# Scores in float32r from high parts and rests, with the maxima subtracted by a product with ones, in an attention block between two feed-forward layers

## The chip, the cores and the metric

The kernel runs on one core of a Trainium2 chip, as one program. The metric is the device time of one execution in microseconds. The core has five engines that run beside each other, each through its own instructions in order: TensorE (PE, matrix products, with weight loads PEld), VectorE (DVE), ScalarE (ACT), GpSimd (POOL) and SyncE (SP), which here only issues DMA transfers. They wait for each other, and where need be for themselves, through counting semaphores. Products go to PSUM; everything else lies in SBUF, 128 partitions wide.

Times on the page and below are those of one profiled execution; the medians are over several runs without a profiler.

## What is computed

The input x is 16 batches of 256 tokens of 256 features, in float32. A feed-forward layer with ternary weights, an attention layer with 16 heads of 16 dimensions and rotary positions, and the feed-forward layer again are added to it:

```python
q = (x @ Wq.T).reshape(B, S, N_HEADS, HEAD_DIM).transpose(0, 2, 1, 3)
...
q = _apply_rope(q)
k = _apply_rope(k)
scores = jnp.einsum('bhqd,bhkd->bhqk', q, k) / np.sqrt(HEAD_DIM).astype(np.float32)
scores = jnp.where(causal, scores, -jnp.inf)
attn = jax.nn.softmax(scores, axis=-1)
out = jnp.einsum('bhqk,bhkd->bhqd', attn, v)
...
x = x + 0.5 * _L0_ffn_ref(_layernorm(x, axis=-1), ...)
x = x + _L0_attn_ref(_layernorm(x, axis=-1), L0_attn_Wq, L0_attn_Wk, L0_attn_Wv, L0_attn_Wo)
x = x + 0.5 * _L0_ffn_ref(_layernorm(x, axis=-1), ...)
```

The weights of q and k are drawn with a large factor, so scores are large, and the softmax needs its maxima subtracted and its scores nearly at float32's precision.

## The kernel before, in words

**Stages.** x stays in SBUF throughout (`xs`). `ffn(0, ...)` runs the first layer in 66 steps of four tiles of tokens. Then the attention runs batch by batch, and `ffn(2, ...)` is the second layer. The feed-forward products already use float32r: an operand is split into a high part that float32r holds exactly and a rest, and each is multiplied in turn (`turn_in`, `up`, `down`).

**Order.** The order of all work is written out by hand: `InOrder` (L188) keeps each engine's instructions in the order of the program, so nearly all of the profile's lines read L196. A batch of attention is eight calls of `slot(b, p)`, p from 0 to 7 (L687), one for each pair of heads. In each slot several batches are in work: `scores(bw, p, bm, p ^ 1)` computes the weights' scores of batch b - 1 (`w`) and, for the maxima, those of batch b (`m`). Batch b + 1 is being projected and rotated (`project_qk`, `rotate`, on POOL), older ones are multiplied with the values (`attend`), divided and projected out. Batch 0's slots lie among the last steps of the first feed-forward layer; a last loop (L815) computes w alone for batch 15, while the second layer begins.

**Scores.** Each score is computed twice. `m` has queries on PSUM's partitions; on it, VectorE's reduction (L592) finds each query's maximum over the allowed keys, with the sign turned, into one column of `maxes`, and drops the masked scores themselves into a scratch tile `masked` of the pool `proj`, which has two buffers of it. A reduction is two instructions: the operation and a read of the accumulator. `w` has keys on the partitions; it becomes exp(scores) after VectorE has added a causal mask (L608) and ScalarE has taken the exponential (L611). m takes one PSUM bank for each of a slot's two heads, from a pool of two; w takes two banks of a pool of two times two.

**Layout of q and k.** The head's 16 dimensions stand in a group of 32 rows, so that a product uses a quarter of TensorE's rows, and four heads' products may stand beside each other. `spread` (L504) copies a rotated q or k into its 32 rows through ScalarE with a column of zeros and ones as scale: heads of even and odd groups use the lower and the upper 16 rows. One of the unused rows carries the maxima: k has ones there (`one`), and q the negated maximum, put there by two transfers after `turn_max` (L528) has turned `maxes` with TensorE and copied it to `mT`. So the product of 32 rows is score minus maximum at once. These are float32 products, which TensorE takes in several passes; the trace shows two instructions for each.

**Queues.** SP issues, for each batch, two transfers for each of two halves that swap neighbouring rows for the rotation (`pair` from `raw`, L493) and two for each half's maxima (L537). POOL multiplies by cosine and sine, adds (L496 to L502), prepares the next batch's normalized x (`ready_x`, in p = 7) and multiplies by the reciprocal sums (`divide`, in p = 1 and p = 5), whose result `o` VectorE transposes a slot later (`turn_out`).

Of the kernel before, what the change touches and what calls it, by code (L numbers as in the profile page):

```python
# [23 lines left out]
S = 256  # L24
# [6 lines left out]
def kernel(  # L31
# [38 lines left out]
    w2q = const.tile([P, NFC, D], FR, name="w2q")  # L70


    wqk = const.tile([P, KC, 2, 2, 4, 2, HD], FP, name="wqk")
# [28 lines left out]
    for k in range(KC):  # L102
        rows = slice(k * P, (k + 1) * P)
        nc.sync.dma_start(out=wv[:, k, :], in_=wqkvT[rows, 2 * D :])
        for at in range(0, 2 * D, 4 * HD):
            n, j, e = at // D, at // P % 2, at // (4 * HD) % 2
            nc.sync.dma_start(
                out=wqk[:, k, n, j, :, e, :],
                in_=wqkvT[rows, at : at + 4 * HD].rearrange("p (r d) -> p r d", d=HD),
            )  # L110
    for at in range(0, P, HD):
        r, n = at // 32, at // HD % 2
# [7 lines left out]

    ident = const.tile([P, P], FP, name="ident")
    make_identity(nc, ident)

    averaging = const.tile([P, P], FP, name="averaging")
    nc.gpsimd.memset(averaging, 1.0 / (D * FF))
# [51 lines left out]

    maxes = [state.tile([P, 2, 2, P], FP, name=f"maxes_{i}") for i in range(2)]  # L180
    for v in maxes:
        nc.gpsimd.memset(v, 0.0)


    mv = [state.tile([P, NTILE, 2], FP, name=f"mv_{i}") for i in range(3)]
# [85 lines left out]
    cosT = const.tile([P, S], FP, name="cosT")  # L271
    sinT = const.tile([P, S], FP, name="sinT")

    own = [const.tile([P, 1], FP, name=f"own_{e}") for e in range(2)]
    one = [const.tile([P, 1], FP, name=f"one_{e}") for e in range(2)]

    def make_tables():
        tp = ps_mm.tile([P, 2, S], FP, name="mm")
        for n, table in enumerate((cos_sb, sin_sb)):
            wide = small.tile([P, 2, P // HD, HD], FP, name="wide", bufs=2)  # L280
            gpsimd.tensor_copy(wide, table.unsqueeze(2).to_broadcast([P, 2, P // HD, HD]))
            for c in range(2):
                tensor.transpose(
                    tp[:, n, c * P : (c + 1) * P],
                    wide[:, c, :, :].rearrange("p h d -> p (h d)"),
                    ident,
                )
        scalar.copy(cosT, tp[:, 0, :])
        scalar.copy(sinT, tp[:, 1, :])
        columns = ident.rearrange("p (r e d) -> p r e d", e=2, d=HD)  # L290
        for e in range(2):
            vector.tensor_reduce(own[e], columns[:, :, e, :], AX.XY, ALU.add)
            vector.tensor_reduce(one[e], columns[:, :, 1 - e, 0:1], AX.XY, ALU.add)

# [150 lines left out]
        later.extend(todo)  # L445


    xn_a, xnT, qT, kT, o, oT, y_a = {}, {}, {}, {}, {}, {}, {}
    pT, sums = {}, {}


# [2 lines left out]
        for k in (0, 4 * S)  # L454
    )
    qk = [flat2[:, at : at + 2 * S].rearrange("p (n s) -> p n s", n=2) for at in (0, 2 * S)]

    def ready_x(b, engine=gpsimd):
        xn_a[b] = pp.tile([P, 2, D], FP, name="xn_a", bufs=1)
# [16 lines left out]
    def project_qk(b, j, first=0, end=4):  # L476

        if first == 0:
            begun[b, j] = ps_mm.tile([P, 2, S], FP, name="mm")
        to = begun[b, j]  # L480
        for n, k in [(n, k) for n in range(2) for k in range(KC)][first:end]:
            tensor.matmul(
                to[:, n, :],
                wqk[:, k, n, j].rearrange("p r e d -> p (r e d)"),
                xnT[b][:, k, :],
                start=(k == 0),
                stop=(k == KC - 1),
            )
# [12 lines left out]
        if 2 in parts:  # L501
            gpsimd.tensor_add(qk[j], qk[j], pair[j])  # L502

    def spread(b, j, e):  # L504


        if (j, e) == (0, 0):
            qT[b] = hp.tile([P, 4, S], FP, name="qT", bufs=3)
            kT[b] = hp.tile([P, 4, S], FP, name="kT", bufs=3)
        g = 2 * j + e  # L510
        scalar.activation(qT[b][:, g, :], qk[j][:, 0, :], AF.Identity, scale=own[e])
        scalar.activation(
            kT[b][:, g, :], qk[j][:, 1, :], AF.Identity, bias=one[e], scale=own[e]
        )

    def project_v(b, c):
        v = ps_mm.tile([P, D], FP, name="mm")
# [7 lines left out]
            )  # L525
        scalar.copy(vals[b % 2][:, c, :, 0:HD], v.rearrange("p (h d) -> p h d", d=HD))

    def turn_max(b, j):  # L528

        tp = ps_mm.tile([P, S], FP, name="mm")  # L530
        for c in range(2):
            tensor.transpose(tp[:, c * P : (c + 1) * P], maxes[b % 2][:, c, j, :], ident)
        mT = hp.tile([P, S], FP, name="mT")
        scalar.copy(mT, tp)
        for e in range(2):
            rows = slice(HD * (1 - e), P, 32)
            sync.dma_start(out=qT[b][rows, 2 * j + e, :], in_=mT[rows, :])  # L537

    def scores(bw, pw, bm, pm):

# [12 lines left out]
        if masked:  # L553
            for j in range(2):
# [5 lines left out]
                    stop=False,  # L560
                    skip_group_check=True,
                )
        for c in range(2):
            for j in range(2):
                if w is not None:
                    h = 2 * pw + j
                    rows, g = slice(32 * (h % 4), 32 * (h % 4) + 32), h // 4
                    tensor.matmul(
                        w[:, j, c * S : S + c * P],
                        kT[bw][rows, g, c * P : (c + 1) * P],  # L570
                        qT[bw][rows, g, c * P : S],
                        start=(c == 0 and not masked),
                        stop=(c == 1),
                        skip_group_check=masked,
                    )
                if m is not None:
                    h = 2 * pm + j
                    rows, g = slice(32 * (h % 4), 32 * (h % 4) + 32), h // 4
                    tensor.matmul(
                        m[j][:, c * P : c * P + (c + 1) * P],  # L580
                        qT[bm][rows, g, c * P : (c + 1) * P],
                        kT[bm][rows, g, 0 : (c + 1) * P],
                        start=(c == 0),
                        stop=(c == 1),
                    )
        if m is not None:
            for j in range(2):
                h = 2 * pm + j
                at = 32 * (h % 4) + HD * (1 - h // 4 % 2)
                for c in range(2):  # L590
                    cols = (c + 1) * P
                    vector.tensor_tensor_reduce(  # L592
                        out=pp.tile([P, S], FP, name="masked")[:, 0:cols],
                        in0=m[j][:, c * P : c * P + cols],
                        in1=mask_q[:, S - cols : S],
                        scale=-1.0,
                        scalar=-MASKED,
                        op0=ALU.add,
                        op1=ALU.min,
                        accum_out=maxes[bm % 2][:, c, h // 8, at : at + 1],  # L600
                    )

        def weigh():
# [11 lines left out]
    def attend(b, half):  # L615

        av = ps_mm.tile([P, 2, S], FP, name="mm")
        for n in range(2):
            g = 2 * half + n
            for c in range(2):  # L620
                for r in range(4):
                    tensor.matmul(
                        av[32 * r : 32 * r + 32, n, c * P : S],
                        vals[b % 2][:, c, 4 * g + r, :],
                        pT[b, 2 * g + r // 2][:, r % 2, c * S : S + c * P],
                        start=(c == 0),
                        stop=(c == 1),
                    )
        sums[b, half] = av
# [57 lines left out]
    def slot(b, p, more=lambda: None):  # L687
# [25 lines left out]
            rotate(up, p // 2 - 1, *((1, 2) if p % 2 else (0,)))  # L713
        if p == 4 and past is not None:
            attend(past, 0)
        if p == 6 and b + 2 < NB:
            turn_x(b + 2)
        if p == 7:
            if last is not None and b < NB - 1:
                project_out(last, range(1, 2))  # L720
            if b + 2 < NB:
                project_qk(b + 2, 0, 0, 1)
            if b + 3 < NB:
                ready_x(b + 3)
            if up is not None:
                spread(up, 0, 0)
        more()
        weigh()
        for n, half, at in ((last, 1, p), (past, 0, p - 4)):
# [24 lines left out]
        50: lambda: (rotate(0, 1, 0), spread(0, 0, 0)),  # L754
        52: lambda: (rotate(0, 1, 1), spread(0, 0, 1)),
        55: lambda: rotate(0, 1, 2),
        56: lambda: ready_x(2, vector),
    }
    HEAD = 59
# [28 lines left out]
    for p in range(8):  # L788
# [11 lines left out]


    ahead = {
        0: lambda: project_out(NB - 3),
        1: lambda: turn_max(z, 1),
    }
    behind = {
# [77 lines left out]
```

## Time and profile before

| | us |
|---|---|
| median of 3 runs | 599.89 |
| lowest and highest | 598.81, 600.18 |
| the profiled execution | 599.31 |
| its span on the page | 597.5 |
| first feed-forward layer alone | from the start to about 140 |
| reductions of the maxima, batch 0 | 141.4 to 163.9 |
| reductions of the maxima, batches 1 to 15 | 164.6 to 447.7 |
| second feed-forward layer | from about 448 on |

The core's TensorE clock is granted in full throughout (the row PEclk is 9 in all slices, the windows say 1.00).

The costliest groups of the parts that the change touches, each as count, total us and mean ns of one (the page's part 5, with different shapes kept apart):

| engine and operation | count | us | mean ns |
|---|---|---|---|
| DVE reduction, masked from m, 128x256 | 240 | 100.7 | 420 |
| DVE reduction, masked from m, 128x128 | 240 | 68.0 | 283 |
| DVE read of the accumulator into maxes | 512 | 42.4 | 83 |
| PE matmul w from qT, kT, 32 rows, 256 columns | 512 | 91.9 | 426 |
| PE matmul w from qT, kT, 32 rows, 128 columns | 512 | 51.2 | 270 |
| PE matmul m from kT, qT, 256 columns | 480 | 75.5 | 377 |
| PE matmul m from kT, qT, 128 columns | 480 | 62.9 | 321 |
| ACT activation, kT | 64 | 37.9 | 593 |
| ACT activation, qT | 64 | 32.3 | 504 |
| POOL multiplication by cosT, 128x512 | 32 | 41.3 | 1289 |

How to read it: a matmul's time is from its start to a modelled end, and those that follow start long before; for what a block of matmuls takes, look from its first start to the start of what comes next. On VectorE too an operation may start before the one ahead has written its last element. "Idle before" in a group is the time in which its engine had nothing, and the name behind the arrow is what ended it.

### The profile page before, as it was taken

Reading aid. Unit: us, or ns where it says so; the run is one execution under the profiler, and the core shown is the slowest. Engines: PE = TensorE matmul, PEld = TensorE weight load, DVE = VectorE, ACT = ScalarE, POOL = GpSimd, SP = SyncE. Lnnn points to the kernel's source line nnn. Section 1 sums busy time; section 2 is a strip of 40 time slices with the busy share of each in tenths; the row PEclk is TensorE's granted clock in tenths of the full one; section 3 lists DMA queues with packets and bytes.
Section 4 is the critical chain, followed back from the end, with each engine's and each line's share of the span. In section 5 each row is a group of like instructions: output and inputs, shape, how many; then the busy total and the mean of one; then the engine's idle time right before and its main releaser. Section 6 shows DMA issues by size and latency. Waiting matters only on the chain.

```text
span 597.5 us, 14414 instructions
## 1 busy us (share of the span) xinstructions
PE 580.0 (97%) x5398; PEld 467.2 (78%) x5398; DVE 473.5 (79%) x1690; ACT 391.1 (65%) x668; POOL 324.8 (54%) x301
## 2 busy tenths in 40 slices
PE   4999999999999999999999999999999999999996
PEld 3798989887777777777777777777767788888886
DVE  6877888677688999899899999999986466666743
ACT  4576666675476666766667676676765666666664
POOL 4645665693555576555855668464821454455452
PEclk9999999999999999999999999999999999999999
DMA  8810000000010011100110001100000011111101
GB/s 282 196 27 2 1 1 1 36 1 19 19 39 20 20 38 37 37 23 20 38 38 28 31 19 38 38 20 28 31 4 2 2 36 36 36 36 36 35 30 41
DMA packets 25588, 21.26 MB, mean 36 GB/s; under 512 B 11056, under 2 KB 21168, under 8 KB 25520
## 3 DMA queue, kind: packets, MB, share of 16 engines
q1 hardware_dynamic: 24960, 19.44, 10.3%
q8 instruction: 42, 0.69, 0.5%
q10 hardware_dynamic: 560, 0.92, 0.4%
q14 instruction: 26, 0.21, 0.1%
HBM read 7.51 MB, written 4.19 MB: 20 GB/s over the span
## 4 chain that ended last, share of the span: by engine, by line
PE 88%; DVE 5%; ACT 3%; issue 1%; DMA 1%; POOL 1%; DVEq 0%; SPq 0%; POOLq 0%; ACTq 0%
PE mm L196 35%; PE w L196 31%; PE m L196 23%; DMA w<-in_w1T_dram 1%; DVE xn L196 1%; ACT h_high L196 1%; DVE masked L196 1%; ACT h_whole L196 1%; DVE w2q L196 1%; DVE h_rest L196 1%; DVE w L196 1%; DVE st L196 0%; POOL h_rest L196 0%; DVE x L196 0%; ACT pT L196 0%
## 5 line engine op out<-in xcount | busy, mean ns | idle before, releaser
L196 DVE CUSTOM_DVE_ANT_0 masked<-m,mask_q 128x128 f32<-128x128 f32 x480 | 142.1, 351 | 20.6 <-PE m L196 19.7
L196 PE MATMUL m<-xnT,w1q 128*128 128x512 f32 x504 | 143.3, 405 | 0.9 <-ACT xnT L196 0.7
L196 ACT ACTIVATE pT<-w 128x768 f32<-128x768 f32 x128 | 104.1, 814 | 56.3 <-DVE w L196 55.9
L196 ACT ACTIVATE h_high<-m,b_sb 128x512 fp32r<-128x512 f32 x126 | 86.7, 688 | 79.4 <-PE m L196 79.3
L196 DVE TENSOR_TENSOR h_rest<-h_whole,h_high 128x512 fp32r<-128x512 f32 x83 | 74.7, 900 | 60.3 <-ACT h_whole L196 59.9
L196 PE MATMUL w<-w2q,h_high 128*128 128x256 f32 x480 | 120.7, 285 | 0.3 <-DVE w2q L196 0.3
L196 PE MATMUL w<-qT,kT 32*128 32x256 f32 (+1 forms) x1024 | 120.5, 348 | 0.0
L196 PE MATMUL w<-w2q,h_rest 128*128 128x256 f32 x480 | 118.0, 279 | 0.8 <-POOL h_rest L196 0.7
L196 PEld LDWEIGHTS w<-qT,kT 32*128 32x128 f32 x1024 | 90.3, 184 | 33.6 <-issue 22.8
L196 PE MATMUL m<-kT,qT 32*128 32x128 f32 x960 | 115.0, 349 | 0.3 <-ACT kT L196 0.3
L196 POOL TENSOR_TENSOR h_rest<-h_whole,h_high 128x512 fp32r<-128x512 f32 x45 | 60.1, 1335 | 85.3 <-ACT h_whole L196 85.1
L196 PEld LDWEIGHTS m<-xnT,w1q 128*128 128x128 f32 x504 | 87.4, 191 | 16.4 <-DVE xnT L196 2.9
L196 PEld LDWEIGHTS w<-w2q,h_rest 128*128 128x128 f32 x480 | 90.4, 188 | 5.9 <-POOL h_rest L196 1.2
L196 PEld LDWEIGHTS w<-w2q,h_high 128*128 128x128 f32 x480 | 90.3, 188 | 5.0 <-DVE w2q L196 0.8
L196 DVE TENSOR_TENSOR w<-w,mask_k 128x512 f32<-128x512 f32 x123 | 85.5, 695 | 3.7 <-PE w L196 3.6
L196 ACT ACTIVATE h_whole<-m,b_sb 128x512 f32<-128x512 f32 x126 | 85.8, 681 | 0.0
L196 POOL TENSOR_TENSOR o<-avs,inv 128x256 f32<-128x256 f32 x32 | 20.3, 635 | 91.6 <-DVE inv L196 91.6
L196 PE MATMUL mm<-xnT_a,wqk 128*128 128x256 f32 x256 | 68.5, 392 | 0.0
L196 PEld LDWEIGHTS m<-kT,qT 32*128 32x128 f32 x960 | 66.2, 185 | 1.5 <-ACT kT L196 0.7
L196 POOL TENSOR_TENSOR w<-w,cosT 128x512 f32<-128x512 f32 x32 | 41.3, 1289 | 27.0 <-ACT kT L196 13.4
L196 PEld LDWEIGHTS mm<-xnT_a,wqk 128*128 128x128 f32 x256 | 45.8, 189 | 10.0 <-issue 1.3
L196 POOL TENSOR_TENSOR w<-w,sinT 128x512 f32<-128x512 f32 x32 | 40.9, 1277 | 20.4 <-DMA w<-w 20.4
(92 smaller groups left out, 885.8 us busy)
## 6 DMA issues: line engine op xcount, KB each, us to landing
w<-w SPq DMA_DIRECT2D x64, 128.0 KB
out_dram<-x SPq DMA_DIRECT2D x15, 256.0 KB
x<-in_x_dram SPq DMA_DIRECT2D x7, 512.0 KB
w<-in_w2T_dram SPq DMA_DIRECT2D x1, 1024.0 KB
qT<-mT SPq DMA_DIRECT2D x64, 4.0 KB
w<-in_w1T_dram SPq DMA_DIRECT2D x1, 512.0 KB
w<-in_w1T_dram ACTq DMA_DIRECT2D x1, 512.0 KB
wqk<-in_wqkvT_dram SPq DMA_DIRECT2D x16, 32.0 KB
```

The lines of the kernel that those rows point to most:

```text
L196: return tc.keep_in_program_order(getattr(self.engine, name)(*args, **kwargs))
```

## The change

Queries and keys are rotated as before, and then split: `part` makes a high part in float32r and the rest (ScalarE a copy, POOL a subtraction), in a tile of four slots: q high, k high, k rest, q rest. `place` moves them by four transfers into `qkT`, where a head's 32 rows alternate between high part and rest of its 16 dimensions: three planes, a key, a query and the query with high part and rest swapped. The product of key and query is high by high plus rest by rest; that of key and swapped query adds the two mixed ones. Both are float32r. For w a third product adds the negated maxima: a matrix of ones in the head's own rows (`ones`) by `mT`, in which two rows of the head hold the maximum's high part and rest. `part_max` splits the maxima, and `turn_max` turns them with a float32r product with `ident_r`, straight into `mT`; the transfers of the maxima into q go away, and so do `spread`, `own` and `one`.

The scores' products of a slot are issued in an order written out by kind and head. The maxima are kept in a smaller tile. The order of the rows of Wq and Wk is now the natural one, so their load takes four transfers instead of sixteen. The scratch tile `masked` has one buffer instead of two.

```diff
+    ident_r = const.tile([P, P], FR, name="ident_r")
+    nc.gpsimd.tensor_copy(ident_r, ident)
...
-    maxes = [state.tile([P, 2, 2, P], FP, name=f"maxes_{i}") for i in range(2)]
+    maxes = [state.tile([P, 2, 2, 4, 2], FP, name=f"maxes_{i}") for i in range(2)]
+    parts = state.tile([P, 2, 4, 16, 2], FR, name="parts")
...
+    split = [
+        state.tile([P, 4, S], FR, name="split"),
+        flat2[:, 4 * S :].rearrange("p (n s) -> p n s", n=4).bitcast(FR),
+    ]
...
-    def spread(b, j, e):
...
+    def part(b, j):
+        high = split[j][:, 0:2, :]
+        scalar.copy(high, qk[j])
+        gpsimd.tensor_sub(split[j][:, 3:1:-1, :], qk[j], high.bitcast(FP))
+
+    def place(b, j):
+        qkT[b, j] = hp.tile([P, 2, 3, S], FR, name=f"qkT_{j}")
+        for e in range(2):
+            rows = slice(64 * e, 64 * e + 64)
+            for h, slots in enumerate((slice(0, 3), slice(3, 0, -1))):
+                sync.dma_start(
+                    out=qkT[b, j][h::2, e, :, :].bitcast(FP),
+                    in_=split[j][rows, slots, :].bitcast(FP),
+                )
...
+    def part_max(b, j):
+        of = maxes[b % 2][:, :, j, :, :]
+        high, rest = (parts[:, :, :, 0:2, n] for n in range(2))
+        scalar.copy(high, of)
+        gpsimd.tensor_sub(rest, of, high.bitcast(FP))
...
     def turn_max(b, j):
-            tensor.transpose(tp[:, c * P : (c + 1) * P], maxes[b % 2][:, c, j, :], ident)
-        mT = hp.tile([P, S], FP, name="mT")
-        scalar.copy(mT, tp)
-        for e in range(2):
-            rows = slice(HD * (1 - e), P, 32)
-            sync.dma_start(out=qT[b][rows, 2 * j + e, :], in_=mT[rows, :])
+            tensor.matmul(
+                tp[:, c, :],
+                parts[:, c, :, :, :].rearrange("p r d n -> p (r d n)"),
+                ident_r,
+                start=True,
+                stop=True,
+            )
+        mT[b, j] = hp.tile([P, 3, P], FR, name=f"mT_{j}", bufs=1)
+        scalar.copy(mT[b, j][:, 0:2, :], tp)
+        scalar.copy(mT[b, j][:, 2, :], tp[:, 1, :])
...
     def scores(bw, pw, bm, pm):
...
+                todo["w", j] = [
+                    (
+                        w[:, j, 0 : S + P],
+                        ones[e][rows, :],
+                        mT[bw, h // 8][rows, :, :].rearrange("p c q -> p (c q)"),
+                    )
+                ] + [
+                    (w[:, j, c * S : S + c * P], key[:, c * P : (c + 1) * P], moving[:, c * P : S])
+                    for c in range(2)
+                    for moving in (query, swapped)
+                ]
...
+                todo["m", j] = [
+                    (
+                        m[j][:, c * P : c * P + (c + 1) * P],
+                        still[:, c * P : (c + 1) * P],
+                        key[:, 0 : (c + 1) * P],
+                    )
+                    for c in (1, 0)
+                    for still in (query, swapped)
+                ]
+        for kind, n in zip("wmmwmwmww", (0, 0, 1, 1, 2, 2, 3, 3, 4)):
             for j in range(2):
...
+                if (kind, j) in todo:
+                    to, still, moving = todo[kind, j][n]
...
                     vector.tensor_tensor_reduce(
-                        out=pp.tile([P, S], FP, name="masked")[:, 0:cols],
+                        out=pp.tile([P, S], FP, name="masked", bufs=1)[:, 0:cols],
...
-                        accum_out=maxes[bm % 2][:, c, h // 8, at : at + 1],
+                        accum_out=maxes[bm % 2][:, c, h // 8, h % 4, h // 4 % 2 : h // 4 % 2 + 1],
...
     def slot(b, p, more=lambda: None):
...
+        for n, j, at in ((now, 0, 4), (past, 1, 0)):
+            if n is not None and p == at:
+                part_max(n, j)
+        if up is not None and p in (4, 6):
+            part(up, p // 2 - 2)
+        if up is not None and p == 5:
+            place(up, 0)
+        if now is not None and p == 0:
+            place(now, 1)
...
-        for n, at in ((up, {7: (0, 1)}), (now, {2: (1, 0), 3: (1, 1)})):
-            if n is not None and p in at:
-                spread(n, *at[p])
```

More of the change, by code (lines that the diff above doesn't have):

```diff
@@ L70 @@
     w2q = const.tile([P, NFC, D], FR, name="w2q")
-    wqk = const.tile([P, KC, 2, 2, 4, 2, HD], FP, name="wqk")
+    wqk = const.tile([P, KC, 2, 2, P], FP, name="wqk")
     wv = const.tile([P, KC, D], FP, name="wv")
@@ L104 @@
         nc.sync.dma_start(out=wv[:, k, :], in_=wqkvT[rows, 2 * D :])
-        for at in range(0, 2 * D, 4 * HD):
-            n, j, e = at // D, at // P % 2, at // (4 * HD) % 2
+        for n in range(2):
             nc.sync.dma_start(
-                out=wqk[:, k, n, j, :, e, :],
-                in_=wqkvT[rows, at : at + 4 * HD].rearrange("p (r d) -> p r d", d=HD),
+                out=wqk[:, k, 1 - n, :, :],
+                in_=wqkvT[rows, n * D : (n + 1) * D].rearrange("p (j f) -> p j f", j=2),
             )
@@ L176 @@
         nc.gpsimd.memset(v[:, :, :, HD : HD + 1], 1.0)
-    maxes = [state.tile([P, 2, 2, P], FP, name=f"maxes_{i}") for i in range(2)]
-    for v in maxes:
-        nc.gpsimd.memset(v, 0.0)
+    maxes = [state.tile([P, 2, 2, 4, 2], FP, name=f"maxes_{i}") for i in range(2)]
+    parts = state.tile([P, 2, 4, 16, 2], FR, name="parts")
+    nc.gpsimd.memset(parts.bitcast(FP), 0.0)
     mv = [state.tile([P, NTILE, 2], FP, name=f"mv_{i}") for i in range(3)]
@@ L272 @@
     sinT = const.tile([P, S], FP, name="sinT")
-    own = [const.tile([P, 1], FP, name=f"own_{e}") for e in range(2)]
-    one = [const.tile([P, 1], FP, name=f"one_{e}") for e in range(2)]
+    ones = [const.tile([P, P], FR, name=f"ones_{e}") for e in range(2)]
     def make_tables():
@@ L289, in make_tables @@
         scalar.copy(sinT, tp[:, 1, :])
-        columns = ident.rearrange("p (r e d) -> p r e d", e=2, d=HD)
+        columns = ident.rearrange("p (r d n) -> p r d n", r=4, n=2)
         for e in range(2):
-            vector.tensor_reduce(own[e], columns[:, :, e, :], AX.XY, ALU.add)
-            vector.tensor_reduce(one[e], columns[:, :, 1 - e, 0:1], AX.XY, ALU.add)
+            one = small.tile([P, 1], FP, name="one", bufs=2)
+            vector.tensor_reduce(one, columns[:, :, e, :], AX.XY, ALU.add)
+            vector.tensor_copy(ones[e], one.to_broadcast([P, P]))
     LATE = 2
@@ L445, in after_first @@
         later.extend(todo)
-    xn_a, xnT, qT, kT, o, oT, y_a = {}, {}, {}, {}, {}, {}, {}
+    xn_a, xnT, qkT, o, oT, y_a = {}, {}, {}, {}, {}, {}
     pT, sums = {}, {}
@@ L483, in project_qk @@
                 to[:, n, :],
-                wqk[:, k, n, j].rearrange("p r e d -> p (r e d)"),
+                wqk[:, k, n, j, :],
                 xnT[b][:, k, :],
@@ L502, in rotate @@
             gpsimd.tensor_add(qk[j], qk[j], pair[j])
-    def spread(b, j, e):
[L507 to L514, printed above, removed]
+    def part(b, j):
[11 more added lines that the diff above has]
+                )
     def project_v(b, c):
@@ L526, in project_v @@
         scalar.copy(vals[b % 2][:, c, :, 0:HD], v.rearrange("p (h d) -> p h d", d=HD))
+    def part_max(b, j):
[3 more added lines that the diff above has]
+        gpsimd.tensor_sub(rest, of, high.bitcast(FP))
+    mT = {}
     def turn_max(b, j):
-        tp = ps_mm.tile([P, S], FP, name="mm")
+        tp = ps_mm.tile([P, 2, P], FP, name="mm")
         for c in range(2):
-            tensor.transpose(tp[:, c * P : (c + 1) * P], maxes[b % 2][:, c, j, :], ident)
-        mT = hp.tile([P, S], FP, name="mT")
-        scalar.copy(mT, tp)
-        for e in range(2):
-            rows = slice(HD * (1 - e), P, 32)
-            sync.dma_start(out=qT[b][rows, 2 * j + e, :], in_=mT[rows, :])
+            tensor.matmul(
[8 more added lines that the diff above has]
+        scalar.copy(mT[b, j][:, 2, :], tp[:, 1, :])
     def scores(bw, pw, bm, pm):
@@ L562, in scores @@
                 )
-        for c in range(2):
+        todo = {}
+        for j in range(2):
+            if w is not None:
+                h = 2 * pw + j
+                rows, e = slice(32 * (h % 4), 32 * (h % 4) + 32), h // 4 % 2
+                of = qkT[bw, h // 8][rows, e, :, :]
+                key, query, swapped = (of[:, n, :] for n in range(3))
+                todo["w", j] = [
[9 more added lines that the diff above has]
+                ]
+            if m is not None:
+                h = 2 * pm + j
+                rows, e = slice(32 * (h % 4), 32 * (h % 4) + 32), h // 4 % 2
+                of = qkT[bm, h // 8][rows, e, :, :]
+                key, query, swapped = (of[:, n, :] for n in range(3))
+                todo["m", j] = [
[7 more added lines that the diff above has]
+                ]
@@ L564, in scores @@
+        for kind, n in zip("wmmwmwmww", (0, 0, 1, 1, 2, 2, 3, 3, 4)):
             for j in range(2):
-                if w is not None:
-                    h = 2 * pw + j
-                    rows, g = slice(32 * (h % 4), 32 * (h % 4) + 32), h // 4
+                if (kind, j) in todo:
+                    to, still, moving = todo[kind, j][n]
                     tensor.matmul(
[L569 to L584, printed above, removed]
+                        to,
+                        still,
@@ L585, in scores @@
+                        moving,
+                        start=(n == 0 and not (kind == "w" and masked)),
+                        stop=(n == len(todo[kind, j]) - 1),
+                        skip_group_check=True,
                     )
@@ L588, in scores @@
                 h = 2 * pm + j
-                at = 32 * (h % 4) + HD * (1 - h // 4 % 2)
                 for c in range(2):
@@ L724, in slot @@
                 ready_x(b + 3)
-            if up is not None:
-                spread(up, 0, 0)
         more()
@@ L753 @@
         48: lambda: rotate(0, 0, 2),
-        50: lambda: (rotate(0, 1, 0), spread(0, 0, 0)),
-        52: lambda: (rotate(0, 1, 1), spread(0, 0, 1)),
-        55: lambda: rotate(0, 1, 2),
+        50: lambda: (part(0, 0), rotate(0, 1, 0)),
+        51: lambda: place(0, 0),
+        52: lambda: rotate(0, 1, 1),
+        53: lambda: rotate(0, 1, 2),
+        54: lambda: part(0, 1),
         56: lambda: ready_x(2, vector),
@@ L802 @@
     ahead = {
-        0: lambda: project_out(NB - 3),
+        0: lambda: (project_out(NB - 3), part_max(z, 1)),
         1: lambda: turn_max(z, 1),
```

## The prediction

> **What bounds the kernel now.** I read the page first: engines, then the chain that ended last. The chain is TensorE's almost alone, and three kinds of matmul share it; the scores stand in the names w and m.
>
> ```profile
> PE 580.0 (97%) x5398; PEld 467.2 (78%) x5398; DVE 473.5 (79%) x1690; ACT 391.1 (65%) x668; POOL 324.8 (54%) x301
> ...
> PE 88%; DVE 5%; ACT 3%; issue 1%; DMA 1%; POOL 1%; DVEq 0%; SPq 0%; POOLq 0%; ACTq 0%
> ```
>
> Then the windows, because shares are means over stages. In the attention stage TensorE reads as full, but VectorE is not far behind.
>
> ```profile
> 255.00:295.00 40.00, 40.00 (x492) 30.31 (x491) 37.39 (x176) 26.87 (x49) 24.84 (x24) 1.00 0.08 30
> 295.00:335.00 40.00, 39.98 (x484) 30.12 (x485) 36.66 (x173) 27.33 (x50) 25.78 (x26) 1.00 0.08 29
> ```
>
> The columns are the window, then busy us of PE, PEld, DVE, ACT, POOL. DVE has 37.39 of 40: 93%. So I read one slot (p = 2) of VectorE's timeline, and the view of the tile `masked`: these reductions run from 164.6 to 447.7 us, those of the last batch from 431.1.
>
> ```profile
> 303.73 0.29 DVE L196 CUSTOM_DVE_ANT_0 masked<-m,mask_q 128x128 f32<-128x128 f32 x1 [0.62 <-PE m L196]
> 303.95 0.08 DVE L196 DVE_READ_ACCUMULATOR2_ANT maxes<- 128x1 f32 x1
> 303.95 0.42 DVE L196 CUSTOM_DVE_ANT_0 masked<-m,mask_q 128x256 f32<-128x256 f32 x1
> 304.29 0.09 DVE L196 DVE_READ_ACCUMULATOR2_ANT maxes<- 128x1 f32 x1
> 304.29 0.29 DVE L196 CUSTOM_DVE_ANT_0 masked<-m,mask_q 128x128 f32<-128x128 f32 x1
> 304.50 0.08 DVE L196 DVE_READ_ACCUMULATOR2_ANT maxes<- 128x1 f32 x1
> 304.50 0.42 DVE L196 CUSTOM_DVE_ANT_0 masked<-m,mask_q 128x256 f32<-128x256 f32 x1
> 304.85 0.08 DVE L196 DVE_READ_ACCUMULATOR2_ANT maxes<- 128x1 f32 x1
> 304.85 0.70 DVE L196 TENSOR_TENSOR w<-w,mask_k 128x512 f32<-128x512 f32 x1
> 305.45 0.44 DVE L196 STREAM_TRANSPOSE oT<-o 128x256 f32<-128x256 f32 x1
> ...
> 307.81 0.42 DVE L196 BATCH_NORM_STATS2 st<-x 128x6 f32<-128x256 f32 x1
> 308.26 0.18 DVE L196 BATCH_NORM_AGGREGATE mv<-st 128x2 f32<-128x6 f32 x1
> ```
>
> Three things are to be seen. Each reduction starts 0.07 to 0.08 us before the one ahead of it ends (303.95 against 303.73 + 0.29). The aggregate, which must wait for VectorE's own statistics, starts 0.03 us after their end (307.81 + 0.42 = 308.23, then 308.26). And reductions plus mask addition take 305.45 - 303.73 = 1.72 us of every slot.
>
> From 164.6 to 431.1 lie 112 slots (batches 1 to 14): 2.38 us each, 19.04 a batch of 8. VectorE's need in one batch, start to start: 8 x 1.72 = 13.76; two transposes of sums at 0.63 (0.71 less the overlap of 0.08), two of the output at 0.36, two reciprocals at 0.16, two additions at 0.31; statistics at 0.64, about three in four batches, 0.47. Together 17.2 us. The slack against TensorE is 1.8 us a batch, 0.23 a slot.
>
> **The change part by part.** *TensorE's scores, shorter.* Now a w head streams 384 columns in four passes, 1536; at 0.417 ns a column (a 128x256 float32r product starts every 0.117 us, 0.107 of it columns) that is 0.64 us. The block takes from 302.76 to 303.63, 0.87; so 0.23 is start and drain. Afterwards a w head streams 384 (maxima) + 2 x 256 + 2 x 128 = 1152 columns, 0.48, and an m head 768, 0.32, beside it in other row groups: block 0.71, 0.16 saved; m is complete some 0.3 us sooner after the block's start. No row shows a float32r product of 128 columns. Bounds: one pass, 0.053 us (the rate of the 256-column row), or four, 0.213 (the float32 row now). I take one pass, nearest in kind; the other end is a rival.
>
> *VectorE's reductions, longer.* The tile `masked` goes from two buffers to one. In the built program each reduction waited for the count raised by the accumulator read of the reduction two before it, long done; now it waits for that of the one just before. Price: from a start 0.08 before the end to one 0.03 after it, 0.11 to 0.12, for three of a slot's four (the first comes after the mask addition). The wait ahead of a head's first reduction stands in an instruction of its own, since it also waits for TensorE; the trace has such pairs, the waiting one 0.02 and the next 0.045 later: 0.05 more. Bounds for a slot: 0 (if it overlaps as now) and 0.42; the row of the aggregate is the same situation, so I take 0.40. Behind the waiting reduction stand, in order, the mask addition (ScalarE's exponentials wait for it) and the next TensorE block, whose m tiles have one set of two buffers.
>
> The Trainium skill speaks against this price: "VectorE: DVE Perf Modes", section "The DRAIN you can't avoid", has a semaphore after each of eight copies cost nothing more than one after the last. By it the 0.40 would be zero and the time that of the first rival below. The statistics pair of this trace says otherwise, and I go by the row.
>
> *Slot by slot.* VectorE's need becomes 17.2 + 8 x 0.40 = 20.4 a batch, over the 19.04 that a batch takes now. The other loop, m ready to m free: release to block 0.14, m 0.32 and drain 0.2, reductions 1.20 + 0.40, is 2.26 a slot, under the mean of 2.55. TensorE: slot p = 1 is its longest, 2.58 now, 2.42 after, over VectorE's 1.72 + 0.16 + 0.40 = 2.28 there: 0.1 a batch. Batch 20.5, that is +1.46, times 14: +20.4 us.
>
> *Outside these batches.* Batch 0 has only m scores, beside the first FFN, where VectorE has 18.14 of 25 us busy: block 0.64 to 0.32 saves up to 8 x 0.32 = 2.6, less what the waits take back (up to 8 x 0.4): I take -1.5. The last eight slots have only w: 8 x 0.16 = -1.3. Batch 15 lacks the mask addition in five slots, so its waits lie in idle time: 0, at most 8 x 0.1.
>
> *ScalarE* loses eight spreads a batch (4 x 0.50 + 4 x 0.59 = 4.4 us) and gains two 128x512 copies at 0.59, two of 128x16 (0.2, by the 128x1 activation) and two of 128x128 (0.27, on the line through 0.38 at 256 and 0.59 at 512): -2.3. It is 67% busy and waits for VectorE: nothing.
>
> *POOL* gains two 128x512 subtractions at 1.34 and two small ones at 0.2 to 0.4: from 11.8 (24.84 of 40) to 15 us in a batch of 20. Its crowd is p = 3 to 5: four multiplications, two additions (1.28 each), then the first subtraction and the small one, all ahead of `o`. From the sine product, 1 us into p = 3, that is 2 x 1.28 + 1.28 + 0.3 + 1.34 + 2 x 1.28 + 0.62 = 8.7, so `o` is there 2.1 us into p = 6, some 0.7 before VectorE's transposition wants it. Nothing; without that cover up to 0.7 a batch.
>
> *SP* loses four 4 KB transfers a batch (0.58 us of issue each) and gains eight of 192 KB. A pair of 128 KB issued at 303.30 let POOL go on at 306.03: 2.7 us. By bytes a pair of 192 KB takes 4.1. The first pair is issued after POOL's subtraction, about 1.5 us into p = 5, and read at the next p = 0, 6 us later; its second pair two slots after that. The second set, issued at p = 0, is read at p = 4. The exchange of p = 1 queues behind it by 4 x 0.58 = 2.3 us from p = 0 on, less than a slot. Nothing; the start's 16 weight transfers become 4, long before their use.
>
> Sum against the profiled 599.31 us (its span 597.5; the median of the runs is 599.89): +20.4 - 1.5 - 1.3 = +17.6, 616.9. I say 617.
>
> **The rivals.**
> - The waits are free, VectorE overlaps as now. For it: reductions do overlap today; against it: the statistics pair. Then slots are p = 0 and 4 VectorE's 2.35, p = 1 2.42, five others about 2.20: 18.1 a batch, -0.9 x 14 = -13; outside -2.8: 583. It wins as long as the waits cost under 0.24 us a slot: 17.2 + 0.1 + 8 x 0.24 = 19.2, and 14 x 0.2 equals the 2.8 saved outside. Chance 0.12.
> - A float32r product of 128 columns takes four passes, 0.213. Against it: the 256- and 512-column rows show one pass; for it: no such product runs now. Then m needs 2 x 256 + 2 x 512 = 1536 columns, 0.64, the loop of m is 2.6 in the five shorter slots, p = 1 is 2.74, p = 0 and 4 2.75: 21.2, +2.2 x 14 = 31; the last stage +1.3, batch 0 nothing: 632. Chance 0.13.
> - POOL or the new transfers come late once a batch, as POOL is 75% busy in bursts: 1 us x 14 on top of the forecast, 631. For it the 0.7 us of cover; against it that VectorE, not POOL, sets the pace. Chance 0.06.
>
> **How the numbers follow.** The forecast, VectorE as the bound, has 0.69. Its own range, with 0.30 to 0.45 a slot, is 607 to 624. For 8 in 10 I reach to the two slow cases and leave out the fast one: 601 to 632. About 0.2% (1.2 us) can be told from no change. Faster 0.13 (the first rival and an edge of the forecast), same 0.04, slower 0.83.
>
> **What would show it.** Right: the reductions of a slot start 0.04 us after the end of the one ahead and span 1.5 to 1.6 us from the first to the last read, not 1.20; DVE idle waits on "PE m" nearly vanish; TensorE gets gaps ahead of m that end with VectorE; the score block is near 0.7. Wrong: reductions still overlap (then faster), or m products of 128 columns start 0.2 apart (then slower still), or `oT` waits for POOL.

## The result and the profile after

The kernel became slower: 642.34 us in the median (636.94 to 650.95) against 600.03 (598.81 to 600.59) for the kernel before on the same chip. The ratio is 1.062, with an interval of 1.059 to 1.065. The upper two of its four executions, 648 and 651, ran at a lower mean TensorE clock (0.963 and 0.958 instead of 0.982), as did one of `a_two` below (689 at 0.755), and the ratio and all that follows go by the others, here 636.94. The profiled execution is one of these; its span is 635.0 us, against 597.5.

The page first: engines, the row of the granted clock over 40 slices of 15.9 us, and the chain that ended last.

```profile
PE 599.3 (94%) x5654; PEld 478.6 (75%) x5654; DVE 503.7 (79%) x1690; ACT 362.3 (57%) x636; POOL 369.9 (58%) x365
...
PEclk9999999999689999999999999999999999999999
...
PE 51%; DVE 28%; issue 12%; POOL 4%; DMA 3%; ACT 2%; DVEq 0%; SPq 0%; POOLq 0%; ACTq 0%
```

The chain was 88% TensorE's; now 28% is VectorE's, and 12% is time in which an engine waited for nothing that the profile shows. POOL is busy for 45 us more, ScalarE for 29 us less. TensorE is busy for 19 us more, although its scores are shorter; the clock row gives a reason for a part of it: two slices read 6 and 8. The windows there and in the steady part (columns as before: us, then PE, PEld, DVE, ACT, POOL, then clock, DMA share, GB/s):

```profile
158.00:162.00 4.00, 2.84 (x26) 2.37 (x26) 3.02 (x18) 0.60 (x3) 3.83 (x4) 1.00 0.34 73
162.00:179.00 17.00, 17.00 (x110) 12.93 (x112) 10.58 (x47) 6.55 (x12) 7.17 (x7) 0.50 0.38 93
...
255.00:295.00 40.00, 38.84 (x480) 28.08 (x480) 36.50 (x159) 20.70 (x41) 27.55 (x28) 1.00 0.41 104
```

Two readings. From 162 to 179 us the clock is half, and TensorE gets 110 matmul instructions done where the kernel before had 189 in the same window. In the steady part TensorE has gaps (38.84 of 40 instead of 40.00), and VectorE is busy for less than before (36.50 instead of 37.39), which looks as if neither were full; the next view shows what VectorE's other 3.5 us are. The DMA share is 0.41 instead of 0.08.

VectorE's timeline of one slot (p = 0 of batch 8) shows why:

```profile
320.05 0.28 DVE L199 CUSTOM_DVE_ANT_0 masked<-m,mask_q 128x128 f32<-128x128 f32 x1
320.25 0.08 DVE L199 DVE_READ_ACCUMULATOR2_ANT maxes<- 128x1 f32 x1
320.37 0.42 DVE L199 CUSTOM_DVE_ANT_0 masked<-m,mask_q 128x256 f32<-128x256 f32 x1
320.72 0.08 DVE L199 DVE_READ_ACCUMULATOR2_ANT maxes<- 128x1 f32 x1
320.95 0.29 DVE L199 CUSTOM_DVE_ANT_0 masked<-m,mask_q 128x128 f32<-128x128 f32 x1
321.16 0.08 DVE L199 DVE_READ_ACCUMULATOR2_ANT maxes<- 128x1 f32 x1
321.28 0.42 DVE L199 CUSTOM_DVE_ANT_0 masked<-m,mask_q 128x256 f32<-128x256 f32 x1
321.63 0.08 DVE L199 DVE_READ_ACCUMULATOR2_ANT maxes<- 128x1 f32 x1
321.63 0.69 DVE L199 TENSOR_TENSOR w<-w,mask_k 128x512 f32<-128x512 f32 x1
```

Read the starts. Before, a reduction began with the accumulator read ahead of it (303.95 and 303.95). Now it begins 0.12 us after that read's start (320.25, then 320.37), 0.04 after its end; for the second head 0.23 (320.72, then 320.95). From the first start to the last read's end it is 321.71 - 320.05 = 1.66 us; before, 304.93 - 303.73 = 1.20. The mask addition, which waits for nothing here, still begins with the last read (321.63). The gaps between a read's end and the next reduction's start are 0.04, 0.15 and 0.04 us, 0.23 in a slot; over the some 15 slots of the window 255 to 295 that is 3.5 us, all of VectorE's idle time there. So with its waits for itself VectorE is full. Its waits for `m` from TensorE, 14.2 us from 200 to 430 us before, are down to 0.2.

TensorE's scores did get shorter. The block of the next slot goes from 321.62 to 322.40, 0.78 us instead of 0.87, and its float32r products of 128 columns start 0.06 us apart in each head:

```profile
322.14 0.22 PE L199 MATMUL w<-qkT 32*128 32x128 f32 x2
...
322.20 0.27 PE L199 MATMUL w<-qkT 32*128 32x128 f32 x2
```

Where the 37.5 us of span come from, by the starts of each batch's first reduction in the two traces:

| | before | after | more |
|---|---|---|---|
| start of batch 0 | 141.42 | 143.70 | 2.28 |
| batch 0 | 23.21 | 23.41 | 0.20 |
| batch 1 | 19.71 | 26.65 | 6.94 |
| batch 2 | 19.23 | 22.27 | 3.04 |
| batch 3 | 19.24 | 20.96 | 1.72 |
| batches 4 to 14, each | 18.93 | 20.92 | 11 x 1.99 = 21.89 |
| batch 15, to the first reduction of its last slot | 15.84 | 17.69 | 1.85 |
| all behind it | 150.6 | 150.2 | -0.4 |

### The profile page after: what moved, and what is told of

It reads as the page before. It is cut to its first block, busy times and chain, and to the rows that moved or that the text cites. A ratio compares the mean times of both kernels' runs of the same rounds, so it can differ in the third digit from the quotient of the medians.

```text
span 635.0 us, 15147 instructions
## 1 busy us (share of the span) xinstructions
PE 599.3 (94%) x5654; PEld 478.6 (75%) x5654; DVE 503.7 (79%) x1690; ACT 362.3 (57%) x636; POOL 369.9 (58%) x365
## 4 chain that ended last, share of the span: by engine, by line
PE 51%; DVE 28%; issue 12%; POOL 4%; DMA 3%; ACT 2%; DVEq 0%; SPq 0%; POOLq 0%; ACTq 0%
PE m L199 19%; PE w L199 19%; PE mm L199 13%; DVE masked L199 13%; DVE avs L199 2%; DVE maxes L199 2%; DVE w L199 2%; POOL w L199 1%; DVE h_rest L199 1%; DVE xn L199 1%; DVE oT L199 1%; DMA w<-w 1%; DVE st L199 1%; DVE x L199 1%; DMA w<-in_w1T_dram 1%
## 5 line engine op out<-in xcount | busy, mean ns | idle before, releaser
L199 DVE CUSTOM_DVE_ANT_0 masked<-m,mask_q 128x128 f32<-128x128 f32 x480 | 169.1, 352 | 34.3 <-PE m L199 7.3
L199 PE MATMUL m<-qkT 32*128 32x256 f32 x960 | 118.8, 302 | 6.4 <-DVE maxes L199 3.8
L199 PE MATMUL w<-w2q,h_rest 128*128 128x256 f32 x480 | 120.0, 281 | 1.5 <-DVE h_rest L199 1.0
L199 DVE TENSOR_TENSOR h_rest<-h_whole,h_high 128x512 fp32r<-128x512 f32 x83 | 76.8, 927 | 56.1 <-ACT h_whole L199 55.5
L199 PEld LDWEIGHTS m<-qkT 32*128 32x128 f32 x960 | 85.1, 188 | 26.9 <-DVE maxes L199 25.5
L199 PE MATMUL w<-qkT 32*128 32x256 f32 (+1 forms) x1088 | 90.6, 285 | 1.3 <-DVE maxes L199 1.2
L199 PEld LDWEIGHTS w<-qkT 32*128 32x128 f32 x1088 | 76.8, 190 | 2.7 <-DVE maxes L199 1.6
L199 PE MATMUL mm<-xnT_a,wqk 128*128 128x256 f32 x256 | 71.3, 404 | 0.0
L199 PE MATMUL w<-mT,ones 32*128 32x384 f32 x256 | 57.4, 444 | 0.4 <-ACT pT L199 0.4
L199 PE MATMUL mm<-pT,vals 128*32 128x256 f32 (+1 forms) x1024 | 50.9, 329 | 3.5 <-DVE x L199 3.5
```

Source lines behind the costliest of these rows:

```text
L199: return tc.keep_in_program_order(getattr(self.engine, name)(*args, **kwargs))
```

## The experiments

All but the second start from the changed kernel or from a variant of it. Each has the kernel before beside it on its chip, at 598.60 us for the first three and at 600.1 to 600.4 for the others.

**Two scratch tiles, and the kernel before with one buffer.** `a_two` has a scratch tile for each of the two widths, so that a reduction waits for the one before the last again. (No run has two buffers of the full tile in the changed kernel.)

```diff
-                        out=pp.tile([P, S], FP, name="masked", bufs=1)[:, 0:cols],
+                        out=pp.tile([P, cols], FP, name=f"masked_{c}", bufs=1),
```

> The changed kernel with two scratch tiles in place of one, so that a reduction waits for the one two before it. Theory (the own waits are the main cost): the first reduction's start to the last read's end falls from 1.66 to 1.20 us, VectorE's need from 20.4 to about 17.2 us a batch, TensorE becomes the bound again with a batch near 18.4 (18.85 before the change), no stretch of half clock; 588 to 600 us. Rival (float32r products, transfers or POOL carry the loss): the reductions get closer but the batch stays near 20.5, 625 us or more.

`b_one` is the kernel before with only its scratch tile reduced to one buffer.

```diff
-                        out=pp.tile([P, S], FP, name="masked")[:, 0:cols],
+                        out=pp.tile([P, S], FP, name="masked", bufs=1)[:, 0:cols],
```

> The kernel before with one scratch tile in place of two, nothing else. Theory: the same 0.46 us more for a slot's four reductions, here in the longer loop of m (release 0.14, m ready 0.97, reductions 1.66 = 2.77 us a slot): a batch of about 22.3 against 18.85, 640 to 660 us in all, perhaps with stretches of half clock. Rival (the waits are hidden in VectorE's idle time): under 605 us.

Measured: `a_two` 609.14 us, ratio 1.018 (1.015 to 1.022), above the range expected; `b_one` 632.99, ratio 1.057 (1.055 to 1.060), below it. One word in the old kernel costs 34.4 us, nearly the whole loss of the change, 36.9. VectorE's timeline of `b_one`:

```profile
320.48 0.29 DVE L196 CUSTOM_DVE_ANT_0 masked<-m,mask_q 128x128 f32<-128x128 f32 x1
320.70 0.08 DVE L196 DVE_READ_ACCUMULATOR2_ANT maxes<- 128x1 f32 x1
320.82 0.42 DVE L196 CUSTOM_DVE_ANT_0 masked<-m,mask_q 128x256 f32<-128x256 f32 x1
321.17 0.08 DVE L196 DVE_READ_ACCUMULATOR2_ANT maxes<- 128x1 f32 x1
321.39 0.29 DVE L196 CUSTOM_DVE_ANT_0 masked<-m,mask_q 128x128 f32<-128x128 f32 x1
```

The same steps of 0.12 and 0.22 us. The loop of m, from which 22.3 us a batch had been expected, doesn't set the pace: a batch is 21.0, and from 255 to 295 us VectorE is busy for 36.44 of 40 and waits for its own reads in 3.2 of the rest. `b_one` has the old, longer score block, yet its batches 4 and 5 are 20.77 and 20.78 us, near the 20.49 and 20.50 of the changed kernel: once VectorE waits for itself, the rest of the change is worth 0.3 us a batch there, and 0.1 in the mean of batches 4 to 14.

Without the waits the changed kernel still isn't faster than before. Its slots p = 0 to 3 are 2.35, 2.20, 2.27 and 2.28 in batch 6 (before 2.35, 2.53, 2.36, 2.36), and that batch is 17.96 us. But in batches 3, 7 and 9 to 14, p = 5 takes 2.9 to 6.2 us instead of 2.16. POOL's and SP's timeline of `a_two` ahead of the longest one, with TensorE's product that waits:

```profile
321.49 5.82 SPq L199 DMA_DIRECT2D w<-w  x4
...
325.95 1.28 POOL L199 TENSOR_TENSOR w<-w,sinT 128x512 f32<-128x512 f32 x1 [2.61 <-DMA w<-w]
327.31 1.28 POOL L199 TENSOR_TENSOR w<-w,w 128x512 f32<-128x512 f32 x1
328.68 0.19 POOL L199 TENSOR_SCALAR var<-mv 128x2 f32<-128x2 f32 x1
328.96 0.73 POOL L199 TENSOR_TENSOR rstd<-var,power 128x2 f32<-128x2 f32 x1
329.66 1.27 POOL L199 TENSOR_TENSOR w<-w,cosT 128x512 f32<-128x512 f32 x1
330.89 0.22 POOL L199 TENSOR_TENSOR parts<-maxes,parts 128x16 fp32r<-128x16 f32 x1
...
331.16 0.65 PE L199 MATMUL mm<-ident_r,parts 128*128 128x128 f32 x2 [2.58 <-POOL parts L199]
```

`parts` takes 0.22 us, but stands behind five instructions of POOL, the first of which waited 2.61 us for an exchange of neighbouring rows; TensorE's `turn_max`, and all scores behind it, wait for it. From 200 to 430 us TensorE waits for `parts` seven times, 12.3 us in all; in the changed kernel three times, 2.2 us.

**The clock.** `a_fill` adds four projection products, whose results nothing reads, to each of the slots 4 to 7 of batch 0, to close TensorE's gaps there.

```diff
+        if b == 0 and p >= 4:
+            filler = ps_m.tile([P, 2, S], FP, name="m")
+            for n in range(2):
+                for k in range(KC):
+                    tensor.matmul(filler[:, n, :], wqk[:, k, n, 0, :], xnT[1][:, k, :], ...)
```

> The changed kernel with four extra products after the scores of slots 4 to 7 of batch 0, whose results nothing reads, to keep TensorE busy where its clock fell. Theory (the half clock from 162 to 193 us costs batches 1 to 3 some 6 to 9 us): the clock stays full there, batch 1 takes 21 to 22 us instead of 26.7, 627 to 632 us. Rival (those batches are slow for other reasons, late transfers or POOL's queue): 635 us or more.

Measured: 636.70 us, no gain. The windows:

```profile
158.00:162.00 4.00, 4.00 (x33) 3.53 (x32) 2.06 (x9) 0.97 (x3) 3.52 (x5) 1.00 0.27 82
162.00:179.00 17.00, 16.72 (x148) 13.43 (x146) 12.11 (x55) 6.43 (x13) 6.21 (x6) 1.00 0.44 104
```

The first of these windows in `b_one`, for comparison:

```profile
158.00:162.00 4.00, 2.77 (x24) 2.22 (x26) 2.80 (x16) 0.37 (x1) 1.82 (x2) 1.00 0.00 1
```

The drop at 162 us is gone, and batch 1 is 21.92 us instead of 26.65. But the start of batch 0 and batch 0 itself are 4.65 us later with the added products, so batch 2 begins at 193.65 instead of 193.76, and batch 15 is 2.0 us longer, with 6.8 us of half clock in it. The expectation of the time fell. The price of the drop in batch 1 comes out as 4.7 us by this run; `b_one`, at full clock there, has 22.11. What brings the drop about stays open: with the gaps filled it is gone, but `b_one` has TensorE busy for only 2.77 of the same 4 us (2.84 in the changed kernel) and keeps the full clock.

**Which queue holds the kernel without waits.** `a_vec` is `a_two` with the subtraction in `part_max` on VectorE instead of GpSimd (`gpsimd.tensor_sub` becomes `vector.tensor_sub`).

> Two scratch tiles, and the rest of the maxima subtracted on VectorE in place of POOL. Theory (with the own waits gone, TensorE waits in p = 5 for the small subtraction that stands on POOL behind sine, additions, statistics and cosine): the p = 5 slots of 3.4 to 6.2 us (batches 3, 7, 9 to 14) fall to about 2.2, some 15 us less than with two scratch tiles alone, 591 to 598 us. Rival (the transfers of q and k are late themselves): p = 5 or p = 6 stays long, 605 us or more.

Measured: 602.75 us, ratio 1.005 (1.003 to 1.008), between the two cases. p = 5 is back at 2.12 us. The stretch is now in p = 4 (about 3.0 in several batches) and p = 6 (up to 4.9); the waits of 200 to 430 us name POOL and its transfers:

```profile
POOL w L199 <- DMA w<-w: 18.8, 12, 2.9
...
DVE oT L199 <- POOL o L199: 8.9, 7, 2.8
```

Two variants of `a_vec` went at the transfers. `a_half` issues the second half of each `place` two slots later; `a_act` issues the exchange from ScalarE's queue, away from the placements.

> As a_vec, and each half's second pair of transfers into qkT issued two slots later, so that the exchange of rows for the rotation does not stand behind four of them. Theory (the exchange lands late, 3.9 against 2.7 us, because it shares the engines with 768 KB issued just ahead): POOL's wait for w<-w falls from 2.6 to about 1.5 us; 2 to 5 us less than a_vec if POOL's chain still sets the pace, the same if TensorE does. Rival: the second pair comes too late for p = 2 and p = 6, slower than a_vec.

> As a_vec, and the exchange of rows issued from ScalarE's queue in place of SP's. Theory (the exchange queues behind the transfers into qkT): POOL waits for w<-w about 1 us as before the change. Cost: four issues of about 0.6 us a batch on ScalarE, which is 60% busy. Between 3 us less and 5 us more than a_vec.

Measured: `a_half` 603.85, not to be told from `a_vec`, with nearly the same waits of POOL for the exchange (21.5 us in the whole trace, 23.4 in `a_vec`). `a_act` 623.98, far outside its range: that wait is still 20.9, and p = 2 and p = 4 grow to 3.0 and 3.6 us, as ScalarE's own queue in `a_act` explains:

```profile
304.32 1.12 ACTq L199 DMA_DIRECT2D w<-w  x2
305.49 0.81 ACT L199 ACTIVATE pT<-w 128x768 f32<-128x768 f32 x1 [1.20 <-DVE maxes L199]
```

The two issues stand between a copy, which ends at 304.29, and an exponential, and hold it up for 1.2 us. (The releaser named is only the last one that the profile knows; the exponential starts as the issues end, 305.44.) That isn't the whole loss: of the 21 us over `a_vec`, 10 have come up by the end of batch 2, ahead of which the clock was half for 17 us in three stretches. Neither way of moving the transfers gained.

Three variants changed the order of POOL's and ScalarE's work. `a_late` issues `part` behind `weigh` in its slot.

> The version with two scratch tiles and the maxima's subtraction on VectorE (602.75 us), with part(up, j) issued at the end of its slot's own work, after weigh, so that ScalarE's copy to split, which waits for GpSimd, no longer stands in front of that slot's exponential. If the remaining stretch of p = 4 (about 3.0 instead of 2.35) and p = 6 (3.2 to 4.9) is the exponential queued behind this copy: 592 to 599 us, and p = 4 and p = 6 near 2.4 and 2.1. If the stretch is GpSimd's o, late at VectorE's transposition in p = 6: only p = 4 shortens, 598 to 603 us. If neither: 602 to 605 us.

`a_ord` adds this to it:

```diff
-        if p in (2, 3, 4, 5) and up is not None:
+        if p in (2, 3, 4) and up is not None:
             rotate(up, p // 2 - 1, *((1, 2) if p % 2 else (0,)))
...
                 (turn_sums, divide, turn_out)[at](n, half)
+        if p == 5 and up is not None:
+            rotate(up, 1, 1, 2)
```

> The same, and in p = 5 GpSimd's multiplication o is issued ahead of the second half's sine product and sum, which wait for the exchange transfer. If o behind that wait is what holds VectorE in p = 6 (DVE oT waits for POOL o 10.5 us in all): this wait goes, p = 6 is near 2.1 in every batch, and the time is 2 to 8 us under the variant with part after weigh. If GpSimd's chain of products, sums and subtractions is simply too long for its transfers' due times: the sum, and with it the second half's part and place, come later by up to 2 us and p = 0 to p = 4 of the next batch stretch; no gain, or slower by up to 5 us.

Measured: `a_late` 614.04, worse than all its three cases. `a_ord` 600.42, 13.6 us less, more than expected, ratio 1.000 (0.998 to 1.002). The waits of 200 to 430 us in `a_late` say which case was overlooked:

```profile
DVE oT L199 <- POOL o L199: 18.8, 12, 2.8
```

ScalarE's copy came later, behind the exponential, so POOL's subtraction came later, and `o` behind it; p = 6 was 3.6 us in nearly every batch. With `o` ahead of the sine product that wait is 1.1 us in the whole trace, and p = 6 is 2.07. The stretch moved to p = 7, where TensorE now waits for the first placement, in `a_ord`:

```profile
349.12 3.27 SPq L199 DMA_DIRECT2D qkT<-split  x4
...
353.66 0.38 PE L199 MATMUL m<-qkT 32*128 32x256 f32 x2 [0.55 <-DMA qkT<-split]
```

So `a_mix` is `a_ord` with the first half's `part` ahead of `weigh` again.

> The variant with o ahead of the second half's products (600.42 us), with the first half's part put back ahead of weigh in p = 4. In that variant the copy to split stands behind an exponential and starts 0.8 us later, the first placement is issued at 349.12 and lands at 353.66, where TensorE's m of the next p = 0 has waited 0.55 us. If the placement of the first half is what remains late in p = 7: these slots (2.65 to 3.75) go to 2.0 to 2.5, and the time is 594 to 599 us. If the exchange and placement transfers, slower beside each other, are late wherever POOL stands: the stretch moves on to p = 4, and the time is 599 to 603 us.

Measured: 597.36 us against 600.17, ratio 0.996 (0.994 to 0.997): 0.4% under the kernel before, in the first of the two ranges. The window of the steady part:

```profile
255.00:295.00 40.00, 39.78 (x528) 31.01 (x526) 38.88 (x186) 24.05 (x46) 30.75 (x28) 1.00 0.45 113
```

VectorE is busy 38.88 of 40 us, more than in any other kernel here. The best batch is 18.04 us, but batches 4 to 14 have a mean of 19.09 (before 18.93), because p = 4 (2.5 to 3.4 us) and in five batches p = 7 (2.9 to 4.1) are still stretched, batches 11 and 13 most (20.31 and 20.87). The gain lies in batch 0 (21.03 instead of 23.21), in batch 1 (18.70 instead of 19.71) and in batch 15 (15.03 instead of 15.84), less 2.6 us of a later start. What stretches just these was not isolated.

## Why the prediction was right or wrong, point by point

The direction and the mechanism held, the size didn't: 617 forecast, 601 to 632 given, 637 in the profiled execution. What failed is the sum: VectorE's wait for itself was put at 0.40 us a slot and is 0.46, and three terms were missed: the half clock, which the sum lacks (about 4.4 us), the start of batch 0 and batch 0 itself (-1.5 said, +2.5 measured), and the waits in batch 15 (0 said, 1.85 measured). Against the working's +17.6 us stand +37.5:

| term of the sum | forecast | measured |
|---|---|---|
| start of batch 0 and batch 0 | -1.5 | +2.5 |
| batches 1 to 3 | 3 x 1.46 = +4.4 | +11.7 |
| batches 4 to 14 | 11 x 1.46 = +16.1 | +21.9 |
| batch 15 | 0 | +1.85 |
| slots with w only, and the rest | -1.3 | -0.4 |

- *VectorE waits for itself, and becomes the bound.* Right, and shown twice: `b_one` adds only this and loses 34 us, `a_two` takes it away and gains 28, the long half clock being gone with it. The Trainium skill's page "VectorE: DVE Perf Modes", section "The DRAIN you can't avoid", has a semaphore after each copy cost nothing. On this chain it costs 0.12 us an instruction, and here the measurement decides.
- *"so I take 0.40".* Under-sized: 1.66 - 1.20 = 0.46 us a slot. The instruction that holds the wait of its own was put at 0.05 more and costs 0.11 more (0.23 against 0.12). Over eight slots this is 0.5 us a batch; clean batches without statistics took 20.5, those with them in p = 3 20.85, where 20.5 had been said for a mean that held both. In batches 4 to 14, which were missed by 5.8 us, the wait gives 5.3 of them, a batch before of 18.93 where 19.04 was the mean over 14 gives 1.2, and longer slots in batches 7, 9, 11 and 13 give 1.9. Together that is more than 5.8, so the rest of the working was 2.6 us too high there, and no run says where.
- *Batches 1 to 14 priced alike.* Wrong for the first three: +11.7 instead of +4.4. `b_one`, whose mean clock is 0.999, has 22.11, 22.08 and 21.31 there, +7.3, which is 2.4 each and of the size of its later batches (+2.1). So 2.9 of the 7.3 that were missing come with the wait alone, 1.4 of them by its size and the rest unexplained. The other 4.4 are about the half clock's, whose price in batch 1 `a_fill` gives as 4.7.
- *The clock.* The working took its full grant over unsaid, and no rival had it. It was the largest term left out.
- *"I take -1.5" for batch 0.* Wrong, and by two causes. The waits take back what the shorter scores give: batch 0 is 23.41, without waits 21.30 (`a_two`), 1.9 under before, near the forecast. And its start is 2.3 us later; it is 2.7 later in `a_two` and 0.2 in `b_one`, so it comes from the change's new work ahead of it and not from the wait. The traces narrow it down: at 123 us VectorE is 0.3 us later than before, at 130 us 1.8, because four normalizations take 4.70 us instead of 3.75 and a subtraction 1.22 instead of 0.66. GpSimd has one subtraction more, into `split`, in that time; whether this slows VectorE was not tried.
- *"so its waits lie in idle time: 0" for batch 15.* Wrong: `b_one` has +2.6 there, `a_two` -0.3. So the waits are not hidden there, though the mask addition is gone in five slots; the forecast's upper end was 0.8.
- *One pass for a 128-column float32r product.* Right: starts 0.06 us apart. That rival fell; the block is 0.78 where 0.71 was said.
- *ScalarE, POOL, SP and the transfers: "nothing".* Nearly true in the changed kernel, where VectorE's slower pace gives them time, and false the moment that cover is gone. Then they cost more than the shorter scores bring: `a_two` is at 609.14, where the rival with free waits had 583. That rival's slots are there (17.96 for its best batch, 18.1 said), but not as a mean. The POOL crowd was counted for `o` alone; the small `parts`, whose row was priced at 0.2 to 0.4 us, was what held TensorE, for 2.58 us ahead of the longest slot.

## What to carry to other kernels

When a tile that nobody reads loses a buffer, its writer can come to wait for itself, as here: ask of every scratch tile which instruction raised the count that the next writer waits for, and count that wait on the engine that is nearly full. If one wait sets the pace, what seems hidden behind it is only untested: price the next limit (here POOL's order and transfers landing) at the pace without the wait. An engine's busy share leaves its waits for itself out, so count the gaps between its own instructions before calling it idle. And look at the granted clock by windows before a difference is put down to the work.

## What was not expected of the hardware

- The clock fell to half in whole steps: 17.07 us from 162.2 and 3.41 us from 189.5 in the changed kernel, 3.4 and 6.8 us in `a_fill`, each near a multiple of 3.41. Ahead of the long drop TensorE was busy for 2.84 of 4 us, with no gap over 0.9 us. The Trainium skill, "TensorE: Matmul & The Clock Gate", section "What's actually happening", gives a window of the same length and half the clock after an idle window; no gap here was that long. Its section "A second HAM failure mode: psum-queue depth-cycling" tells of short idle times between groups of products that made the clock go back and forth. The gaps here are of that kind, and `a_fill`, which fills them, has no drop there; but `b_one`, busy for 2.77 of the same 4 us, kept its full clock, so the busy share alone doesn't decide. What does, no run here shows.
- A wait of VectorE for its own last instruction costs 0.12 us when the waiting instruction holds it, and 0.22 to 0.23 when it stands in an instruction of its own, in both kernels with one buffer.
